# Twelve of sixteen batches with their transposes moved from TensorE to VectorE and DMA, one-instruction masked maxima, and regrouped slots

## The chip, the cores and the metric

The kernel runs on one core of a Trainium2 chip. A core has five instruction queues that run in parallel: TensorE (PE in the profile, with its weight loads as PEld), VectorE (DVE), ScalarE (ACT), GpSimd (POOL) and SyncE (SP). SP computes nothing; it issues the transfers (DMAs), which sixteen DMA engines then carry out. Each queue runs its instructions in the order in which they stand in the program and waits on semaphores for the others. The metric is the time of one execution in microseconds (us); lower is better.

## The reference

One layer is computed for sixteen batches of 256 tokens by 256 features, in float32. Reduced to its steps, per batch:

```
u    = modulate(layer_norm(logmap(x)))            # shift and scale from the condition vector
q,k,v = u @ Wqkv + b, rescaled per head (16 heads of 16 features)
o    = softmax(q k^T) v                           # full attention, 256 x 256 per head
x1   = mobius_add(x, gate * logmap(plin(o, Wo)))
u    = modulate(layer_norm(logmap(x1)));  ff = plin(plin(u, Wf1), Wf2)
xc   = mobius_add(x1, gate * ff)
local  = windowed attention on xc (64-token blocks, each sees itself and the block before)
remote = attention of 8 heads on 64 pooled tokens
xr   = x + (gate_l * local + gate_r * remote) @ Wout
z    = xr scaled per feature, @ W, scaled again
out  = xr + top-2 of 4 experts with low-rank updates on z (1024 hidden features)
```

The softmaxes of the local and the remote attention subtract the row maximum; the masks are additive.

## The kernel before

A batch is two tiles of 128 tokens (partitions) by 256 features. A matrix product needs its left operand with features in the partitions, so each product with a weight matrix is preceded by a transpose of the activation. `front(b)` computes up to `xc`, `back(b, xt, xc)` the rest; sixteen batches are unrolled in full.

**Who sets the order.** Nothing runs while the code is recorded: every call goes through the class `Plan`, which notes the instruction, its tiles and its predecessors as a node. `Plan.emit` then runs a list scheduler (`Plan.schedule`) over all nodes of all batches: each node has a cost from `Plan.cost`, a due time from its batch number times a period, and the scheduler gives each engine at each step the ready node with the earliest start, ties by due time. It also hands out the buffers (slots in SBUF under the tags t1, t2 and t4, eight PSUM banks). The result is a fixed order on each of the five queues, so batches overlap: the instructions of four to five batches stand interleaved. In TensorE's order of 5458 recorded operations, batch 7 reaches from 30% to 61% of the list.

**Transposes.** `turned(src, tag, b)` (line 699) makes four 128x128 TensorE transposes against `ident` into one PSUM bank, and `transposed` (line 708) copies the bank to SBUF, mostly on ScalarE. Per batch this is done eight times: `muT` twice (the two modulated inputs), `kT`, `qT`, `oT`, `xcT`, `locT` and `xrT`. The attention results come out as features by tokens in PSUM; `to_tokens` (lines 806 and 813) copies two banks to SBUF, one on VectorE and one on ScalarE, and transposes them back with eight TensorE transposes, for the full attention (`av`) and for the local one (`al`). The remote attention does the same with one bank and four transposes (lines 1120 and 1124). That is 32 + 16 + 4 = 52 TensorE transposes a batch.

**Local maxima.** For the row maxima of the local attention, TensorE first writes the mask into a bank, as a product of `ident_bf` with `maskq` (line 1046, sixteen a batch), then adds the scores on top of it (line 1048), and VectorE takes the maximum of two heads at a time with one TENSOR_REDUCE (line 1054, sixteen a batch).

**Transfers.** A batch issues 20 DMAs on SP: the input `x`, four pieces of the modulation vector `ada`, the row maxima through DRAM (`mT`: one write at line 1079, six reads at line 1083), the low-rank rows through DRAM (`low`: one write at line 1270, four reads at line 1273), the expert ratio `rho` through DRAM (line 1278 writes 256 elements of four bytes, line 1280 reads them back), and the output. The names carry over to the new kernel.

```
    def turned(src, tag, b):
        ps = bank(f"{tag}_ps_{b}").rearrange("p (c s) -> p c s", c=NC)
        for c in range(NC):
            for t in range(NT):
                pe.transpose(ps[:, c, bass.ts(t, P)], src[:, t, bass.ts(c, P)], ident)
```

Of the kernel before, what the change touches and what calls it, by code (L numbers as in the profile page):

```python
# [34 lines left out]
WIN = 64  # L35
E, R = 4, 4
# [8 lines left out]
N_T1, N_T2, N_T4 = 6, 18, 8  # L45
# [20 lines left out]
class Plan:  # L66
# [5 lines left out]
    PERIODS = 65.0, 70.0, 75.0, 80.0  # L72
    HURRIES = 5.0, 6.0, 7.0, 8.0
    early = ("pqk", "qk2")
    NARROWS = 3, 4

    def __init__(self, tc):
        nc = tc.nc
        self.tc, self.nodes, self.batch, self.hold = tc, [], 0, None
        self.seen, self.slots, self.ring, self.kept, self.wide = {}, {}, {}, set(), set()  # L80
        self.phys, self.place = {}, {}
        self.real = {"pe": nc.tensor, "dve": nc.vector, "act": nc.scalar, "pool": nc.gpsimd, "sp": nc.sync}
# [46 lines left out]
    def region(self, ap, write=False):  # L129
        name, dims = ap.name if isinstance(ap, View) else ap.tensor.name, list(ap.ap)  # L130
        if ap.space == DRAM and write:
            return name, 0, P, ap.offset, ap.offset + 1
        if ap.space in (PSUM, DRAM):
            return name, 0, P, 0, 1 << 30
        step = dims[0][0]
        p0, f0 = divmod(ap.offset, step)
        return name, p0, p0 + dims[0][1], f0, f0 + 1 + sum((n - 1) * st for st, n in dims[1:])

    def note(self, eng, op, args, kw):
# [7 lines left out]
        first = self.region(outs[0])[0]  # L147
# [4 lines left out]
        if not joins:  # L152
            n = dict(
                eng=eng, ops=[], cost=0.0, batch=self.batch, pre=set(), post=set(), tiles=set(),
                id=len(self.nodes), hold=self.hold, first=first, table=None, modes=[],
# [4 lines left out]
        n["cost"] += self.cost(eng, op, outs, rest, n)  # L160
        for write, aps in ((False, rest), (True, outs)):
            for ap in aps:
                if is_ap(ap):
                    self.access(n, write, *self.region(ap, write))
# [17 lines left out]
    def cost(eng, op, outs, rest, n):  # L182

        cols = max(int(np.prod(v.shape[1:])) for v in outs + [r for r in rest if hasattr(r, "tensor")])
        if eng == "sp":
            run = min((v.ap[-1][1] if v.ap[-1][0] == 1 else 1 for v in outs + rest if hasattr(v, "tensor")), default=1)
            return 0.1 + int(np.prod(outs[0].shape)) * 4 / (2e5 if run >= 128 else 0.7e5 if run >= 32 else 0.05e5)
        if eng == "pe":
# [8 lines left out]
            if n["hold"] is not None and (lhs.shape[0] < 64 or outs[0].shape[0] < 64):  # L197
                return (0.024 if lhs.shape[0] < 64 else 0.016) + 0.00042 * cols
# [7 lines left out]
        if eng == "pool":  # L206
            if op == "affine_select":
                return 0.2 + 0.00098 * cols
            return 0.76 if ALU.pow in rest else 0.27 + (0.0021 if op == "tensor_tensor" else 0.0009) * cols
        extra = 0.06 * (op == "scalar_tensor_tensor") + 0.05 * (op == "tensor_reduce") + 0.06 * (len(outs) > 1)  # L210
        return max(0.11, 0.05 + 0.0011 * cols + extra)


    def emit(self):
# [5 lines left out]
        for tag, names in self.ring.items():  # L220
            bufs = self.slots[names[0]][1]
            for old, new in zip(names, names[bufs:]):
                behind = [m["id"] for m in users[old]]
                for u in users[new]:
                    if tag in self.early and u["eng"] != "pe":
                        for m in [nodes[m] for m in u["pre"]]:
                            if m["eng"] == "pe" and m["batch"] == u["batch"]:
                                m["pre"].update(behind)
# [5 lines left out]
        lag = lambda n: {"pe": 0.27, "sp": 2.2, "dve": 0.18, "act": 0.18}.get(n["eng"], 0.05)  # L234
# [10 lines left out]
        settings = itertools.product(self.HURRIES, self.PERIODS, self.NARROWS)  # L245
        best = min(settings, key=lambda s: self.schedule(order, users, lag, *s)[0])
        _, out, self.place = self.schedule(order, users, lag, *best)
# [6 lines left out]
    def schedule(self, order, users, lag, hurry, period, most):  # L254
# [16 lines left out]
        held, narrow = set(), 0  # L271
# [4 lines left out]
        table, mode, out = None, None, []  # L276

        def start(n):
# [5 lines left out]
            for tag, names in need.items():  # L284
                if len(pools[tag]) < len(names):
                    return None, need
                if tag == "bank" and names[0] not in self.wide and narrow + len(names) > most:
# [4 lines left out]
        while len(out) < len(nodes):  # L292
            best = None
            for e, ns in avail.items():
                cand = [(max(t, free[e]), n, need) for n in ns for t, need in [start(n)] if t is not None]
# [26 lines left out]
            n["t"], n["end"] = t, end  # L322
            out.append(n)
# [6 lines left out]
            for m in n["post"]:  # L330
                m = nodes[m]
                m["ready"] = max(
                    m["ready"], end + (lag(n) if m["eng"] != e or e == "sp" else 0.08 if e == "dve" else 0.11 if e == "act" else 0.0)
# [8 lines left out]
def adaln_attn_ffn(ctx: ExitStack, tc: tile.TileContext, i: dict, out: bass.AP):  # L342
# [11 lines left out]
    def bank(name):  # L354
        return plan.tile(psum, [P, 512], "bank", name, 8, False)

    def four(name, b):

        banks = [bank(f"{name}{j}_{b}") for j in range(4)]
# [70 lines left out]
    def temp(shape, name, tag, bufs=1):  # L430

        return plan.tile(work, shape, tag, name, bufs, True, 2048)

    condT = const_tile([P, NC, B], "condT")
    load(condT, i["condT"].rearrange("(c p) b -> p c b", p=P))
    bada = temp([B, 6 * D], "bada", "qk2")
    load(bada, i["b_ada"].partition_broadcast(B))
    ada = temp([B, 6, D], "ada", "pqk")
    ada_f = ada.rearrange("b k d -> b (k d)")
    for k in range(3):  # L440
# [3 lines left out]
        load(wada, i["w_ada"][:, cols].rearrange("(c p) f -> p c f", p=P))  # L444
        for c in range(NC):
            pe.matmul(ps[:B, :], condT[:, c, :], wada[:, c, :], start=c == 0, stop=c == NC - 1)
        dve.tensor_tensor(ada_f[:, cols], ps[:B, :], bada[:, cols], ALU.add)
    for k in (1, 4):
        dve.tensor_scalar_add(ada[:, k, :], ada[:, k, :], 1.0)
    sp.dma_start(out=ada_dram, in_=ada_f)  # L450
# [11 lines left out]


    wf1 = temp([P, NC, FF], "wf1", "qk2")
    load(wf1, i["w_f1"].rearrange("(c p) f -> p c f", p=P))
    wf2 = temp([P, NF, D], "wf2", "qk2")
    load(wf2, i["w_f2"].rearrange("(c p) f -> p c f", p=P))
# [4 lines left out]
    for f in range(0, NF, 2):  # L472
        ps = bank(f"wf1T_ps{f}").rearrange("p (f d) -> p f d", f=2)
        for k in range(2):
            for c in range(NC):
                pe.transpose(ps[:, k, bass.ts(c, P)], wf1[:, c, bass.ts(f + k, P)], ident)
# [888 lines left out]
```

## Time and profile before

| | |
|---|---|
| median of three runs | 1300.51 us (1297.3 to 1302.75) |
| the profiled execution | 1302.17 us, its span 1300.4 us |
| granted TensorE clock, mean | 0.972 |
| TensorE busy | 1207.1 us, 93% |
| VectorE busy | 877.3 us, 67% |
| ScalarE busy | 688.2 us, 53% |
| GpSimd busy | 666.2 us, 51% |
| DMA engines busy, mean of 16 | about 12% |

The span runs from the first to the last instruction of the profiled execution; the execution's own time lies 1.8 us above it, and 1.7 us above the median of the runs. Busy time is the time in which an engine has at least one instruction running. The instructions of the output's store are recorded at 277.4, 353.9, 431.5, 500.0, 578.1, 646.6, 724.1, 792.6 and 873.7 us for the first batches, so a batch is finished every 75 us or so in the middle of the run.

### The profile page before, as it was taken

The page shows a single profiled execution, that of the slowest core. Times are in us where ns is not written, and L with a number is a line of the kernel's source. Part 1 is how long each engine was busy: PE and PEld are TensorE (multiplying, and loading weights), DVE is VectorE, ACT ScalarE, POOL GpSimd, SP SyncE. Part 2 cuts the span into 40 slices and gives each one's busy share as a digit, 9 for nine tenths or more (in the row PEclk, how much of TensorE's full clock was granted, in tenths as well). Part 3 has the DMA queues.
Part 4 walks back from the last instruction along what each step waited for, and adds up shares of the span by engine and source line. Part 5 has one row for each costly group of instructions (what it writes and reads, how often), then busy time and mean ns, then how long its engine had stood idle before and what let it go on. Part 6 is the DMA issues. An engine that isn't in the chain of part 4 may idle for free.

```text
span 1300.4 us, 27101 instructions
## 1 busy us (share of the span) xinstructions
PE 1207.1 (93%) x9684; PEld 797.8 (61%) x9684; DVE 877.3 (67%) x2800; ACT 688.2 (53%) x1750; POOL 666.2 (51%) x1677
## 2 busy tenths in 40 slices
PE   4987999999999999999999999999999998979776
PEld 2654565757666576657666576657656665757465
DVE  5747686876869677776869677676968765573331
ACT  1555667547473755647473755646473753724210
POOL 5167566646464564646464564656455462743210
PEclk7998999999999999999999999899999999999897
DMA  6520001010100201010100101020000100000001
GB/s 193 175 61 17 23 7 35 25 29 10 40 14 18 36 17 30 16 36 9 41 14 18 35 18 31 7 43 11 23 23 17 25 2 20 1 15 7 20 2 25
DMA packets 59462, 38.70 MB, mean 30 GB/s; under 512 B 33312, under 2 KB 53792, under 8 KB 59328
## 3 DMA queue, kind: packets, MB, share of 16 engines
q1 hardware_dynamic: 59328, 36.97, 11.6%
q8 instruction: 76, 1.25, 0.5%
q14 instruction: 58, 0.48, 0.1%
HBM read 31.60 MB, written 5.36 MB: 28 GB/s over the span
## 4 chain that ended last, share of the span: by engine, by line
PE 65%; DVE 11%; POOL 10%; ACT 6%; DMA 4%; issue 3%; SPq 0%; DVEq 0%; ACTq 0%; POOLq 0%
PE bank L784 11%; PE bank L1298 6%; PE bank L904 5%; PE bank L840 5%; PE bank L891 4%; PE bank L699 4%; PE bank L939 4%; PE bank L1048 3%; PE bank L1289 2%; PE bank L1211 2%; PE bank L1153 2%; POOL t L566 2%; PE bank L1046 2%; PE bank L974 2%; ACT t L662 2%
## 5 line engine op out<-in xcount | busy, mean ns | idle before, releaser
L566 POOL TENSOR_SCALAR_AFFINE_SELECT t<-t 128x512 f32<-128x512 f32 (+2 forms) x264 | 168.2, 661 | 37.7 <-ACT t L1174 36.8
L662 ACT ACTIVATE t<-t 128x256 f32<-128x256 f32 x224 | 92.8, 423 | 148.0 <-DVE t L733 53.4
L911 ACT ACTIVATE t<-bank 128x512 f32<-128x512 f32 x256 | 132.3, 615 | 38.8 <-PE bank L904 38.6
L784 PE MATMUL bank<-wot,t 128*128 128x256 f32 x512 | 129.2, 394 | 2.1 <-POOL t L1311 1.9
L1054 DVE TENSOR_REDUCE maxima<-bank 128x2 f32<-128x384 f32 (+1 forms) x256 | 119.9, 482 | 15.1 <-PE bank L1048 15.0
L1298 PE MATMUL bank<-t,wi 128*128 128x256 f32 x512 | 130.0, 389 | 0.0
L784 PEld LDWEIGHTS bank<-wot,t 128*128 128x128 f32 x512 | 93.2, 192 | 28.0 <-issue 11.8
L1174 ACT ACTIVATE t<-bank 128x320 f32<-128x320 f32 x256 | 92.9, 446 | 19.8 <-PE bank L1166 19.3
L1298 PEld LDWEIGHTS bank<-t,wi 128*128 128x128 f32 x512 | 91.5, 192 | 18.2 <-issue 9.0
L840 PE MATMUL bank<-wqkv,t 128*128 128x512 f32 (+1 forms) x256 | 94.8, 504 | 1.4 <-ACT t L708 1.4
L699 PE MATMUL bank<-ident,t 128*128 128x128 f32 x384 | 61.4, 284 | 18.0 <-DVE t L733 11.7
L904 PE MATMUL bank<-t,t 32*128 32x512 f32 x512 | 75.7, 646 | 0.1
L1311 POOL TENSOR_TENSOR t<-t,t 128x512 f32<-128x512 f32 x32 | 43.3, 1368 | 53.4 <-DVE t L1308 52.3
L891 PE MATMUL bank<-t,vpad 128*32 128x256 f32 x1024 | 68.3, 385 | 0.1
L699 PEld LDWEIGHTS bank<-ident,t 128*128 128x128 f32 x384 | 43.8, 142 | 39.2 <-DVE t L733 13.8
L844 DVE SCALAR_TENSOR_TENSOR pqk<-bank,m1f,bqkv 128x512 f32<-128x512 f32 (+1 forms) x64 | 38.9, 614 | 40.6 <-PE bank L840 31.2
L840 PEld LDWEIGHTS bank<-wqkv,t 128*128 128x128 f32 x256 | 45.7, 193 | 33.0 <-issue 25.2
L1166 PE MATMUL bank<-qk 32*128 32x128 f32 (+1 forms) x1024 | 58.9, 330 | 6.8 <-ACT t L1174 4.8
L1304 ACT ACTIVATE t<-bank 128x512 f32<-128x512 f32 x64 | 36.3, 593 | 53.1 <-PE bank L1298 53.1
L708 ACT COPY t<-bank 128x512 f32<-128x512 f32 x80 | 47.5, 593 | 31.6 <-PE bank L699 31.4
L1308 DVE SCALAR_TENSOR_TENSOR t<-bank,t 128x512 f32<-128x512 f32 x64 | 42.3, 681 | 29.9 <-PE bank L1289 29.7
L1166 PEld LDWEIGHTS bank<-qk 32*128 32x128 f32 x1024 | 45.4, 189 | 27.3 <-issue 12.3
(322 smaller groups left out, 2856.1 us busy)
## 6 DMA issues: line engine op xcount, KB each, us to landing
ada<-ada_dram SPq DMA_DIRECT2D x32, 256.0 KB
x<-in_x_dram SPq DMA_DIRECT2D x16, 256.0 KB
ada<-ada_dram SPq DMA_DIRECT2D x32, 128.0 KB
out_dram<-t SPq DMA_DIRECT2D x16, 256.0 KB
qk<-in_w_f_dram SPq DMA_DIRECT2D x2, 1024.0 KB
t<-low_dram SPq DMA_DIRECT2D x64, 32.0 KB
t<-rho_dram SPq DMA_DIRECT2D x16, 128.0 KB
t<-in_w_ada_dram SPq DMA_DIRECT2D x3, 512.0 KB
```

What stands on the lines that cost most here:

```text
L566: pool.affine_select(out=ap, in_=ap, pattern=pattern, compare_op=ALU.is_ge, fill=fill, base=base, channel_multiplier=cm,)
L662: act.activation(junk, src, AF.Square, accum_out=dst)
L699: pe.transpose(ps[:, c, bass.ts(t, P)], src[:, t, bass.ts(c, P)], ident)
L784: pe.matmul(ps[:, t, :], chunks[c][:, bass.ts(t, P)], weights[:, c, :], start=c == 0, stop=c == n - 1)
L840: pe.matmul(ps[:, :w], uT[:, c, bass.ts(t, P)], wqkv[:, c, a : a + w], start=c == 0, stop=c == NC - 1,)
L891: pe.matmul(avs[c][quad(j), gh, :], vpad[:, kt, head(2 * c + gh, j), :], es[j][:, gh, :], start=kt == 0 and gh == 0, stop=kt == NT - 1, sk ...
L904: pe.matmul(scs[j], kT[quad(j), c, bass.ts(kt, P)], qT[quad(j), c].rearrange("p g s -> p (g s)"), start=True, stop=True,)
L911: act.activation(es[j].rearrange("p g s -> p (g s)"), scs[j], AF.Exp)
L1054: dve.tensor_reduce(mx[:, qt, m0 : m0 + 4 * NC + 1 : 4 * NC], scs[j][:, : 2 * w].rearrange("p (g w) -> p g w", g=2), AX.X, ALU.max,)
L1166: pe.matmul(scs[j][:, a : a + w], k2T[quad(j), g % 2, g // 2, bass.ts(kt, P)], q2T[quad(j), g % 2, g // 2, kt * P : kt * P + w], start=Tru ...
L1174: act.activation(e[:, k, 0:NLOC], scs[2 * pr + k][:, :NLOC], AF.Exp)
L1298: pe.matmul(hs[j][:, f, :], wi[:, c, bass.ts(2 * j + f, P)], zT[:, c, :], start=False, stop=c == NC - 1, skip_group_check=True,)
```

## The change

What it does, in order of size:

1. **Transposes of batches 2 to 13.** For these twelve batches (`APART`) `transposed` no longer calls TensorE. VectorE transposes the tile in 32x32 blocks (one instruction, 128x512), four DMAs (one for each group of 32 partitions) write the blocks to a scratch matrix in DRAM in 128-byte runs, so that they lie in transposed order, and one DMA reads the matrix back into SBUF. `qT` and `xrT` take this way too. `to_tokens` and the remote attention's turn call the new `by_dram` for these batches: one VectorE block transpose straight from the PSUM bank, four DMA writes a bank, and one read for all banks. Batches 0, 1, 14 and 15 keep the TensorE transposes.
2. **Local maxima, in all batches.** The mask product is gone; VectorE makes one `tensor_tensor_reduce` a head and tile (scores plus mask, then maximum), 32 a batch in place of 16 TENSOR_REDUCEs. In the program each of these is two instructions, the main one and one that reads out the accumulator.
3. **Slots.** The input ring grows from 4 to 8 (`N_X`), t2 from 18 to 22 and t4 from 8 to 10 slots; the private rings `pqk`, `qk2`, `xpT`, `gkm`, `gkT`, `xr`, `p1o` and `p2o` are dissolved into these; small tiles have 3 or 6 buffers in place of 2. Products claim the SBUF slot of their result before they start.
4. **The planner.** It knows a DMA's issue cost (0.4 or 0.7 us) apart from its transfer time, allows eight DMAs under way, has other prices for VectorE, GpSimd and quarter-array products, follows regions of tiles more finely, and tries four settings. The DMAs of a batch rise from 20 to 83.

In the new order of TensorE's 4578 recorded operations, batch 7 reaches from 17.5% to 67% of the list.

```diff
+APART = range(2, 14)
-N_T1, N_T2, N_T4 = 6, 18, 8
+N_X = 8
+N_T1, N_T2, N_T4 = 6, 22, 10
...
+    SETTINGS = ((5, 55, 4, 1), (6, 65, 4, 0), (7, 75, 5, 1), (6, 65, 4, 1))
...
         if eng == "sp":
-            run = min((v.ap[-1][1] if v.ap[-1][0] == 1 else 1 for v in outs + rest if hasattr(v, "tensor")), default=1)
-            return 0.1 + int(np.prod(outs[0].shape)) * 4 / (2e5 if run >= 128 else 0.7e5 if run >= 32 else 0.05e5)
+            long = all(v.ap[-1][0] == 1 and v.ap[-1][1] >= P for v in outs + rest)
+            n["move"] = int(np.prod(outs[0].shape)) * 4 / (2.2e5 if long else 1.1e5)
+            return 0.4 if long else 0.7
...
+        if op == "tensor_tensor_reduce":
+            return 0.08 + 0.00105 * cols
...
             for e, ns in avail.items():
-                cand = [(max(t, free[e]), n, need) for n in ns for t, need in [start(n)] if t is not None]
+                since = free[e] if e != "sp" or len(landed) < 8 else max(free[e], landed[-8])
+                cand = [(max(t, since), n, need) for n in ns for t, need in [start(n)] if t is not None]
...
     def transposed(src, tag, b, copy=act.copy):
 
         t = spare([P, NC, S], tag, b)
-        copy(t, turned(src, tag, b))
+        if b in APART:
+            blocks = spare([P, NT, D // PADH, PADH], tag + "b", b)
+            dve.transpose(blocks.rearrange("p t k s -> p (t k s)"), src.rearrange("p t d -> p (t d)"))
+            rows = scratch([D, S], tag, b)
+            for a in range(4):
+                sp.dma_start(
+                    out=rows.rearrange("(k d) (t a s) -> d a t k s", d=PADH, a=4, s=PADH)[:, a],
+                    in_=blocks[quad(a)],
+                )
+            sp.dma_start(out=t, in_=rows.rearrange("(c p) s -> p c s", p=P))
+            return t
+        copy(t, turned(src, tag, b, t))
         return t
...
+    def by_dram(banks, tag, b):
+        n = 4 * len(banks)
+        rows = scratch([2 * S // PADH, PADH, n, PADH], tag, b)
+        for c, ps in enumerate(banks):
+            t = spare([P, 2 * S // PADH, PADH], f"{tag}c{c}", b)
+            dve.transpose(t.rearrange("p k r -> p (k r)"), ps.rearrange("p g s -> p (g s)"))
+            for j in range(4):
+                sp.dma_start(out=rows[:, :, 4 * c + j].rearrange("k s r -> s k r"), in_=t[quad(j)])
+        o = spare([P, 2, NT, n, PADH], tag + "o", b)
+        sp.dma_start(
+            out=o.rearrange("p g t n r -> p (g t) (n r)"),
+            in_=rows.rearrange("(m k) s n r -> (k s) m (n r)", k=4),
+        )
+        return [o[:, :, t].rearrange("p g n r -> p n g r") for t in range(NT)]
+
+    def to_tokens(banks, tag, b, into):
+        if b in APART:
+            return by_dram(banks, tag, b)
...
                 with plan.unit():
-                    for j in range(4):
-                        pe.matmul(scs[j][:, : 2 * w], ident_bf, maskq[:, 2 * a : 2 * (a + w)], start=True, stop=False)
                     for j in range(4):
                         pe.matmul(
                             scs[j][:, : 2 * w], qm[quad(j), c, bass.ts(qt, P)], km[quad(j), c, :, k0 : k0 + w],
-                            start=False, stop=True,
+                            start=True, stop=True,
                         )
                 for j in range(4):
-                    m0 = 4 * c + j
-                    dve.tensor_reduce(
-                        mx[:, qt, m0 : m0 + 4 * NC + 1 : 4 * NC],
-                        scs[j][:, : 2 * w].rearrange("p (g w) -> p g w", g=2), AX.X, ALU.max,
-                    )
+                    for gh in range(2):
+                        m = 4 * (NC * gh + c) + j
+                        dve.tensor_tensor_reduce(
+                            out=seen[:, :w], in0=scs[j][:, gh * w : (gh + 1) * w], in1=maskf[:, a : a + w], scale=1.0,
+                            scalar=NEG, op0=ALU.add, op1=ALU.max, accum_out=mx[:, qt, m : m + 1],
+                        )
...
-        rT = spare([P, LG, S], "avrc", b)
-        dve.tensor_copy(rT, avr)
+        if b in APART:
+            pss = by_dram([avr], "avr", b)
...
-        ps = turned(xr, "xrT", b)
+        if b in APART:
+            ps = xsT = transposed(xr, "xrT", b)
```

## The prediction

> **What bounds the kernel now.** I read the busy shares first, then the slices, then the busy times by stretch, then the groups that the change touches, then SP's queue.
>
> ```profile
> PE 1207.1 (93%) x9684; PEld 797.8 (61%) x9684; DVE 877.3 (67%) x2800; ACT 688.2 (53%) x1750; POOL 666.2 (51%) x1677
> PE   4987999999999999999999999999999998979776
> DVE  5747686876869677776869677676968765573331
> ...
> PE 65%; DVE 11%; POOL 10%; ACT 6%; DMA 4%; issue 3%; SPq 0%; DVEq 0%; ACTq 0%; POOLq 0%
> ```
>
> TensorE is full except at both ends, and 65% of the chain that ended last is TensorE's own work. The stretches (us busy and, in brackets, instructions) show it in numbers:
>
> ```profile
> core 0: us, PE busy (x) PEld busy (x) DVE busy (x) ACT busy (x) POOL busy (x), PEclk, DMA share, GB/s
> 0.00:300.00 300.00, 259.61 (x1894) 161.25 (x1894) 214.00 (x702) 165.65 (x415) 162.41 (x438) 0.95 0.22 62
> 300.00:976.00 676.00, 661.99 (x5472) 436.74 (x5470) 491.94 (x1566) 394.26 (x1013) 377.44 (x954) 0.99 0.11 23
> 976.00:1300.40 324.40, 285.54 (x2322) 199.81 (x2320) 171.38 (x534) 128.29 (x324) 126.31 (x286) 0.94 0.07 13
> ```
>
> The middle 676 us are nine batch periods of 75.1 us (output stores every 75 us). Per period TensorE is busy 73.6 us (98%), VectorE 54.7 (73%), ScalarE 43.8, GpSimd 41.9. The two ends hold the other seven batches' worth of work and 79 us of idle TensorE. So TensorE work removed in the middle is worth its full length, until VectorE, next in line with 20 us to spare, takes over. The groups touched:
>
> ```profile
> L699 PE MATMUL bank<-ident,t 128*128 128x128 f32 x384 | 61.4, 284 | 18.0 <-DVE t L733 11.7 <-DVE m2ay L691 3.3 <-ACT t L881 0.9
> L813 PE MATMUL bank<-ident,t 128*128 128x128 f32 x256 | 40.9, 278 | 0.6 <-ACT t L881 0.5
> L1124 PE MATMUL bank<-ident,t 128*128 128x128 f32 x64 | 12.7, 285 | 0.2 <-DVE t L1120 0.2
> L1054 DVE TENSOR_REDUCE maxima<-bank 128x2 f32<-128x384 f32 x128 | 67.8, 547 | 9.9 <-PE bank L1048 9.9
> L1054 DVE TENSOR_REDUCE maxima<-bank 128x2 f32<-128x256 f32 x128 | 52.1, 417 | 5.2 <-PE bank L1048 5.1
> L806 DVE COPY t<-bank 128x512 f32<-128x512 f32 x32 | 22.1, 691 | 43.0 <-PE bank L891 23.3 <-PE bank L1153 19.8
> ```
>
> Here the first number after the bar is the group's busy time, the second one instruction's length. Last, the transfers: a stretch in which almost only 128-byte runs are moved, one in which one 256 KB input of 1 KB runs is loaded, and SP's wait at the four-byte writes of `rho`:
>
> ```profile
> 430.50:432.00 1.50, 1.50 (x20) 0.57 (x23) 0.88 (x2) 0.52 (x3) 1.05 (x6) 1.00 0.31 50
> 409.00:410.50 1.50, 1.50 (x17) 0.95 (x15) 1.50 (x7) 0.00 (x0) 0.00 (x0) 1.00 0.67 175
> SPq L1280 <- DMA rho_dram<-rtx: 94.0, 15, 8.2
> ```
>
> **The change part by part.** *TensorE, transposes.* Three groups of line 699 (61.4 + 12.8 + 10.6 us for 512) give 0.166 us each; line 813 gives 0.160, line 1124 0.198. A batch of the twelve loses 32 x 0.166 + 16 x 0.160 + 4 x 0.198 = 8.7 us. *TensorE, masks.* Line 1046 is 46.5 us in all, 2.9 us a batch, gone in all sixteen. So TensorE needs 73.6 - 11.6 = 62.0 us for a batch of the twelve and 70.7 for the other four.
>
> *VectorE, block transposes.* Thirteen a batch of 128x512. The trace has this operation at 128x64 only: 0.245 us (the low-rank rows). With the slope of the TENSOR_REDUCE rows, (547 - 417)/128 = 1.02 ns a column, 448 more columns make 0.70 us, as the 512-column copy's 0.69: +9.1 us. Gone are four such copies (-2.7); splitting six tiles' products adds about 0.6.
>
> *VectorE, maxima.* No row has this operation. The nearest has two inputs, a 256-column product with an accumulator (line 745), at 0.42 us, followed by an accumulator read of 0.081 us. Down the same slope, 128 columns cost 0.29 and 192 cost 0.35; with the read 0.37 and 0.43. Sixteen of each make 12.9 us against 119.9/16 = 7.5 now: +5.4 us in every batch. From below, without the read, 10.3 (+2.8); from above, two inputs at twice the slope, 17.9 (+10.4). I take +5.4, by the two rows that are nearest. The planner prices the two forms at 0.21 and 0.28 us, so its order leaves VectorE too little room.
>
> Sum for VectorE: 54.7 + 9.1 - 2.7 + 0.6 + 5.4 = **67.1 us** for a batch of the twelve, 60.7 for the others. That passes TensorE's 62.0: the bound moves to VectorE. ScalarE loses five copies of 0.593 and two of 0.587 us, to 39.7; GpSimd stays.
>
> *SP.* 52 writes and 11 reads are added. The low-rank reads, also 32 partitions in 128-byte runs, take 0.604 us to issue, the `mT` write 0.32; inputs 0.39. So 16.6 to 31.4 us for the writes (I take the upper, the like shape) and 4.3 for the reads, beside 9.0 now: 45 us a batch. SP stands still, too: `rho`'s read waits for `rho`'s write, 94.0 us in 15 times, 6.3 each. Before, few were in a hurry behind it; now block writes and reads of other batches are. About 5 us a batch, as a few issues fit in between: 50 of 70 us, not the bound.
>
> *DMA engines.* 13 x 2048 runs of 128 bytes. In the first stretch 50 GB/s x 1.5 us are 75 KB, 586 runs, in 0.31 x 16 x 1.5 = 7.4 engine-us: 12.7 ns a run. That is for reading DRAM; the writes have no row. From above: all 59328 packets of the queue, 11.6% of 16 x 1300 us, mean 40.7 ns. The writes take 26624 x 12.7/16 = 21 us a batch, or 68 at the upper end; thirteen reads of 256 KB cost 0.67 x 1.5 = 1.0 us each; 0.11 x 75 = 8 are there now. So 42 us (89 at the upper end); I take 42, since the 256-byte writes of `mT` let their reads go 1.8 us after issue, no slower than reads.
>
> A rule speaks against this. The Trainium skill, "VectorE: DVE Perf Modes", section "The three transpose paths", says that a plain copy which transposes by strides is 19 times slower than the hardware's transpose; taken at 19 x 1.0 us for each of thirteen tiles that would be an estimated 247 us of DMA a batch, and a time near 3400 us. But there single elements are scattered; here VectorE has turned the 32x32 blocks and the runs stay 128 bytes long. By the rule the prediction fails outright; by the row it stands.
>
> *Latency.* A turn through DRAM takes 0.7 (VectorE) + 2.4 (four issues) + 1.8 (landing, as `mT`) + 0.4 + about 2.2 us (landing of a read) = 7.5, and about 6 more when ten other DMAs stand between on SP, as is typical. Nine such turns follow one another in a batch. What covers it is the order: between a block transpose and the first user of its result stand, in the median by kind of turn, 13 to 34 us of TensorE work and 11 to 38 of VectorE work by the rows above, and each batch now spans half the list. At the shortest distances (4 to 6 us in `alo`, `locT`, `xcT`) an engine will wait. *Slots* cost nothing by themselves: they are what allows eight batches under way. Extra `x` loads at the start lie among 190 GB/s of weight loads.
>
> **The sum.** Middle: nine periods. VectorE at 67.1 us cannot be as full as TensorE was (98%), since TensorE stands at 62.0 beside it and SP's order ties batches together. Bounds: 67.1/0.98 = 68.5, and 75.1 if all is lost. I take 95%, 70.6 us, nearer the first: 9 x 4.5 = 40 us less. Ends: VectorE is idle for 86 and 153 us there, so TensorE still paces them; four batches without the new path gain 2.9 each and three with it 11.6: 46 us less. The idle 79 us stay. 1300.4 - 40 - 46 = 1214; the execution's 1.8 us on top and the 1.7 us by which it lies above the median cancel. **1215 us.** A change within 0.5% (6.5 us) could not be told from none.
>
> **Rivals.** *TensorE stays the bound.* VectorE's 50 us of extra work at the ends fit its idle time; if the order spreads its work so well that the middle runs at TensorE's 62.0/0.98 = 63.3 us, 9 x 11.8 + 46 = 152 less: 1148; at VectorE's mean over all batches, 65.5/0.98 = 66.8, it is 1180. For it speaks the eight-batch depth, against it the planner's low VectorE prices.
>
> *The turns come late.* A stream of 63 more DMAs, held up each batch for about 8 us at `rho`, stalls the engines until the period is 75 again: 1255 if the ends keep their gain, 1300 if the longer batch latency eats that too.
>
> *The short writes bind (slower).* DMA work a batch is 21 us + 1.66 us for each nanosecond of a 128-byte write. It passes VectorE's 67 us at 28 ns and today's 75 at 32 ns. At the 40.7 ns above it is 89 us: 9 x 14 more in the middle, the three batches at the ends +14 each, less 12 from the other four: 1456. For it: four-byte writes hold `rho`'s read 6.3 us for 256 elements, 0.4 us for each of an engine's sixteen. Against it: the 256-byte writes show nothing of the kind, and 128 is nearer to them.
>
> **How the numbers follow.** VectorE-paced 0.50 (1190 to 1250), TensorE-paced 0.22 (1148 to 1190), late turns 0.13 (1250 to 1300, a third of it within 0.5% or above), short writes 0.15 (from 1310 up). The range leaves out most of the last case and the lower end of the second: 1150 to 1310. Faster 0.50 + 0.22 + 0.08 = 0.80, same 0.03, slower 0.17.
>
> **What would show it.** VectorE busy near 1050 us (877 + 16 x 6.0 + 12 x 6.4) and TensorE near 1057 in a span near 1214; the maxima's main instruction at 0.29 and 0.35 us with an accumulator read of 0.08; the block transpose at 0.70; output stores 70 us apart; a DMA share near 0.6 in the middle; a chain in which VectorE has gained on TensorE, with waits for `muT`, `av` and `al` through DRAM of a few us a batch. Block transposes of 0.9 us, maxima of 0.5, a DMA share over 0.9, or TensorE waiting mostly for SP's reads would make it wrong.

## The result, and the profile after

| | before | after |
|---|---|---|
| median of the runs | 1301.45 us | 1382.38 us (1381.05 to 1387.42) |
| ratio, 95% interval | | 1.0635 (1.0598 to 1.0671) |
| span of the profiled execution | 1300.4 us | 1385.7 us |
| granted TensorE clock, mean | 0.972 | 0.909 |
| TensorE / VectorE busy | 1207.1 / 877.3 us | 1201.2 / 984.3 us |

The forecast was 1215 us in a range of 1150 to 1310. The change makes the kernel 6.4% slower: size and sign were wrong.

The page of the changed kernel: busy time, two rows of slices and the chain that ended last.

```profile
PE 1201.2 (87%) x8799; PEld 781.2 (56%) x8804; DVE 984.3 (71%) x3754; ACT 661.3 (48%) x1676; POOL 653.8 (47%) x1677
...
PE   4997977888998988898899889988988989898886
...
DVE  5896898688768879685887869777836385583631
...
q1 hardware_dynamic: 434080, 118.81, 39.2%
...
PE 36%; DVE 28%; DMA 12%; POOL 10%; issue 6%; ACT 6%; SPq 2%; DVEq 0%; ACTq 0%; POOLq 0%
```

The row of nines that TensorE had in the middle is gone, and nothing has taken its place: VectorE stands at 71%, the DMA engines at 39% (the share at the end of the queue's line). The chain passes from engine to engine: TensorE's own work is 36% of it, 65% before. By this page no single engine bounds the kernel; it waits in turn for each.

The same three stretches as in the prediction (the last is longer by the time lost):

```profile
core 0: us, PE busy (x) PEld busy (x) DVE busy (x) ACT busy (x) POOL busy (x), PEclk, DMA share, GB/s
0.00:300.00 300.00, 239.19 (x1460) 138.36 (x1460) 237.06 (x917) 168.77 (x427) 166.90 (x492) 0.88 0.48 121
300.00:976.00 676.00, 608.04 (x4718) 390.03 (x4721) 528.75 (x1981) 347.42 (x889) 349.54 (x885) 0.93 0.49 101
976.00:1386.00 410.00, 353.98 (x2624) 252.84 (x2624) 218.50 (x858) 145.07 (x362) 137.36 (x300) 0.89 0.19 39
```

In the middle TensorE falls from 98% to 90%, VectorE rises to 78%, and the granted clock falls from 0.99 to 0.93. The first output is stored at 359 us (277 before), the second at 476 (354), the eighth at 944 (793): the middle wins nothing back, it loses 29 us more from the second store to the eighth. The last is stored at 1382 us (1297).

I cut TensorE's time into three parts, from its instructions and the clock records of the trace: work at full clock (busy time less half of the busy time that lies in stretches at half clock), what the half clock adds, and idle time up to TensorE's last instruction (the span ends some 4 us later).

| | span | work at full clock | added by half clock | idle |
|---|---|---|---|---|
| before | 1300.4 | 1184 | 23 | 89 |
| after | 1385.7 | 1099 | 102 | 180 |
| difference | +85 | -85 | +79 | +91 |

So the change does take work off TensorE, 85 us of the 151 that the prediction counted (12 x 8.7 + 16 x 2.9), but order and clock cost twice that. The groups that the change made, and the two score groups beside them:

```profile
L1132 DVE CUSTOM_DVE_ANT_0 seen<-bank,maskf 128x128 bf16<-128x128 f32 (+1 forms) x512 | 165.3, 323 | 45.9 <-PE bank L1125 9.5 <-PE bank L1218 0.5 <-DVE maxima L1132 0.2
L976 PE MATMUL bank<-t,t 32*128 32x512 f32 x512 | 92.6, 697 | 19.2 <-DVE t L912 6.0 <-ACT t L951 5.2 <-DVE maxima L1132 4.4
L1125 PE MATMUL bank<-t,t 32*128 32x256 f32 (+1 forms) x512 | 79.3, 512 | 16.9 <-DVE maxima L1132 8.8 <-DVE maxima L1150 3.0 <-ACT t L1300 1.8
L743 DVE STREAM_TRANSPOSE t<-t 128x512 f32<-128x512 f32 x96 | 66.7, 699 | 2.5 <-PE bank L1068 1.2 <-PE bank L1393 0.7
L855 DVE STREAM_TRANSPOSE t<-bank 128x512 f32<-128x512 f32 x60 | 42.5, 708 | 36.8 <-PE bank L961 15.5 <-PE bank L1193 14.5 <-DMA al_dram<-t 3.2
L1132 DVE DVE_READ_ACCUMULATOR2_ANT maxima<- 128x1 f32 x512 | 42.3, 83 | 0.3
```

The prices were right: block transposes 0.70 us, maxima 0.323 in the mean (0.290 and 0.356 by shape) and 0.083 for the accumulator read. In the kernel before the two score groups had these rows:

```profile
L904 PE MATMUL bank<-t,t 32*128 32x512 f32 x512 | 75.7, 646 | 0.1
L1048 PE MATMUL bank<-t,t 32*128 32x256 f32 (+1 forms) x512 | 52.5, 480 | 0.0
```

The rows grew by 16.9 and 26.8 us, some of it by the half clock: together nearly the 46.5 us of the mask products' row. And TensorE now waits 19.2 and 16.9 us before them.

### The profile page after: what moved, and what is told of

Read it like the earlier page. It is cut to its first block, busy times and chain, and to the rows that moved or that the text cites. A ratio compares the mean times of both kernels' runs of the same rounds, so it can differ in the third digit from the quotient of the medians.

```text
span 1385.7 us, 27800 instructions
## 1 busy us (share of the span) xinstructions
PE 1201.2 (87%) x8799; PEld 781.2 (56%) x8804; DVE 984.3 (71%) x3754; ACT 661.3 (48%) x1676; POOL 653.8 (47%) x1677
## 4 chain that ended last, share of the span: by engine, by line
PE 36%; DVE 28%; DMA 12%; POOL 10%; issue 6%; ACT 6%; SPq 2%; DVEq 0%; ACTq 0%; POOLq 0%
PE bank L828 7%; DVE seen L1132 6%; PE bank L1393 5%; PE bank L976 3%; PE bank L1125 3%; DMA t<-xcT_dram 3%; POOL t L605 2%; PE bank L961 2%; DVE t L743 2%; DMA t<-mT_dram 2%; DMA t<-low_dram 2%; PE bank L908 2%; PE bank L1384 2%; DVE t L1402 2%; PE bank L1253 2%
## 5 line engine op out<-in xcount | busy, mean ns | idle before, releaser
L605 POOL TENSOR_SCALAR_AFFINE_SELECT t<-t 128x512 f32<-128x512 f32 (+1 forms) x260 | 166.2, 666 | 92.7 <-ACT t L1261 91.6
L1132 DVE CUSTOM_DVE_ANT_0 seen<-bank,maskf 128x128 bf16<-128x128 f32 (+1 forms) x512 | 165.3, 323 | 45.9 <-PE bank L1125 9.5
L1393 PE MATMUL bank<-t,wi 128*128 128x256 f32 x512 | 121.0, 387 | 0.0
L976 PE MATMUL bank<-t,t 32*128 32x512 f32 x512 | 92.6, 697 | 19.2 <-DVE t L912 6.0
L1125 PE MATMUL bank<-t,t 32*128 32x256 f32 (+1 forms) x512 | 79.3, 512 | 16.9 <-DVE maxima L1132 8.8
L1253 PE MATMUL bank<-t,t 32*128 32x192 f32 (+1 forms) x1024 | 65.4, 352 | 17.7 <-ACT t L1261 6.7
L1253 PEld LDWEIGHTS bank<-t,t 32*128 32x128 f32 x1024 | 50.3, 206 | 44.3 <-issue 15.4
L855 DVE STREAM_TRANSPOSE t<-bank 128x512 f32<-128x512 f32 x60 | 42.5, 708 | 36.8 <-PE bank L961 15.5
L743 DVE STREAM_TRANSPOSE t<-t 128x512 f32<-128x512 f32 x96 | 66.7, 699 | 2.5 <-PE bank L1068 1.2
L1238 PE MATMUL bank<-t,v2pad 128*32 128x128 f32 (+1 forms) x1536 | 54.5, 270 | 9.7 <-POOL t L605 4.2
```

The costliest lines, as they stand in the source:

```text
L605: pool.affine_select(out=ap, in_=ap, pattern=pattern, compare_op=ALU.is_ge, fill=fill, base=base, channel_multiplier=cm,)
L743: dve.transpose(blocks.rearrange("p t k s -> p (t k s)"), src.rearrange("p t d -> p (t d)"))
L976: pe.matmul(scs[j], kT[quad(j), c, bass.ts(kt, P)], qT[quad(j), c].rearrange("p g s -> p (g s)"), start=True, stop=True,)
L1125: pe.matmul(scs[j][:, : 2 * w], qm[quad(j), c, bass.ts(qt, P)], km[quad(j), c, :, k0 : k0 + w], start=True, stop=True,)
L1132: dve.tensor_tensor_reduce(out=seen[:, :w], in0=scs[j][:, gh * w : (gh + 1) * w], in1=maskf[:, a : a + w], scale=1.0, scalar=NEG, op0=ALU. ...
L1253: pe.matmul(scs[j][:, a : a + w], k2T[quad(j), g % 2, g // 2, bass.ts(kt, P)], q2T[quad(j), g % 2, g // 2, kt * P : kt * P + w], start=Tru ...
```

## The experiments

Three things can be blamed: the turns through DRAM, the maxima, and the new planner with its slots, which settles the order on every engine anew. All times below are medians, with the ratio to the kernel before measured beside it (it took 1299 to 1305). A setting of the planner is given as hurry (how heavily waiting times weigh in the due times), period in us, the number of PSUM banks that short products may hold and, in the new planner, how many fewer of them the later batches may.

### The parts, one taken out at a time

x1: the turns out; maxima, planner and slots stay (the planner takes setting 6, 65, 4, 0).

```diff
-APART = range(2, 14)
+APART = range(0)
```

> No batch has its transposes made by VectorE and DMA; the one-instruction maxima, the new slots and the new planner stay (the planner now picks hurry 6, period 65). If the turns through DRAM are what costs the time (late arrivals, and the half clock that follows the gaps), this runs below the kernel before: 1300 minus the 46 us of mask products, about 1255, with a granted clock of 0.96 or more. If the maxima on VectorE are the cause, it stays above 1320. If the new slots and planner are, it stays above 1320 as well, and the first output store stays near 359 us.

1379.91 us, ratio 1.062 (1.059 to 1.065): without the turns the kernel is as slow, at another setting, so the turns alone do not explain the loss.

x2: the maxima out; turns, planner and slots stay (setting 7, 75, 5, 1).

```diff
+                        pe.matmul(scs[j][:, : 2 * w], ident_bf, maskq[:, 2 * a : 2 * (a + w)], start=True, stop=False)
...
-                    for gh in range(2):
...
+                    dve.tensor_reduce(
+                        mx[:, qt, m0 : m0 + 4 * NC + 1 : 4 * NC],
```

> The maxima are made as before (mask product on TensorE, sixteen TENSOR_REDUCEs a batch), the turns through DRAM stay (the planner picks hurry 7, period 75). If the 32 short VectorE instructions that hold the score banks are the cause, about 1240 to 1290 (TensorE has 46 us more work than in the changed kernel, VectorE 88 less). If the turns are, 1370 or more.

1343.31 us, ratio 1.034 (1.026 to 1.041): 39 us better, still worse than before.

x3: both out, so that planner and slots are left. None of the four settings gives a complete order here, so five were added; 7, 75, 3, 0 was taken.

> Neither the turns through DRAM nor the new maxima: the kernel before with the new slots and the new planner alone. None of the four settings gives a complete order here, so five more are offered; the planner picks hurry 7, period 75, three narrow banks. If slots and planner do no harm, 1290 to 1310. If the new order by itself costs time (a late first batch, more gaps), 1330 or more.

1391.12 us, ratio 1.071 (1.067 to 1.074). Of the slots the prediction says that they "cost nothing by themselves"; with the planner that comes with them, this order costs 90 us. Its waits of TensorE (line waited for, releaser: us, times, longest):

```profile
PE bank L1189 <- DMA t<-mT_dram: 27.7, 6, 8.9
PE bank L1258 <- DMA t<-mT_dram: 17.2, 4, 6.7
PE bank L1389 <- DMA t<-low_dram: 16.4, 3, 12.2
```

These transfers were in the kernel before, too, where TensorE waited 17.6 us for `mT` and 10.7 for `low`; in the new order it reaches their users too early and waits 44.9 and 16.4.

x5: after, at the setting that x2 took.

```diff
-    SETTINGS = ((5, 55, 4, 1), (6, 65, 4, 0), (7, 75, 5, 1), (6, 65, 4, 1))
+    SETTINGS = ((7, 75, 5, 1),)
```

> The changed kernel with the planner held to hurry 7, period 75, five narrow banks, in place of the 5, 55, four that it chose: the same instructions in another order. If the choice of the order is what fails (the dues of a 55 us period start eight batches at once, so the first output store comes at 359 us instead of 277), 1230 to 1300 with a first store before 300 us. If the turns or the maxima fail whatever the order, within 2% of 1382.

1401.94 us, ratio 1.079 (1.073 to 1.084). At one and the same setting the maxima cost 59 us over x2.

### The parts put into the kernel before

y1: the new maxima alone, with the old planner and slots (which now takes setting 8, 75, 4).

> The kernel before with the one-instruction maxima alone; old planner, old slots. If the new planner and slots alone make the loss (the kernel before with them took 1391 us), the maxima bring what was forecast for them, less what VectorE's 5.4 us a batch give back: 1250 to 1285. If the maxima hurt in any order, 1300 or more.

1366.23 us, ratio 1.046 (1.041 to 1.052).

y2: the turns alone with the old planner and slots (only one setting, 5, 75, 3, gives an order).

> The kernel before with the turns through DRAM for batches 2 to 13 alone; old planner (it prices the short writes at 70 GB/s and knows no limit of eight DMAs), old slots. If planner and slots make the loss, the turns bring most of the 104 us of TensorE transposes: 1200 to 1245. If the turns come late in any order, 1280 or more.

1582.85 us, ratio 1.212 (1.206 to 1.218).

```profile
PE bank L796 <- DMA t<-locT_dram: 38.9, 8, 8.3
PE bank L1192 <- POOL t L567: 32.3, 30, 5.4
PE bank L796 <- DMA t<-oT_dram: 31.5, 3, 20.5
PE bank L700 <- DVE t L745: 30.3, 7, 12.3
```

With the old slots the turns are plainly late: TensorE waits up to 20.5 us for one of them. So the new slots and planner together make the turns bearable (the prediction gave this to the slots; which of the two does it was not taken apart), but that is not their whole effect.

y3: turns and maxima with the old planner and slots (setting 5, 65, 3).

> Both in the kernel before, with its own planner and slots: the change without its parts 3 and 4. If those two parts make the loss, this is the forecast's own case, with VectorE as the bound: 1150 to 1250. If turns and maxima together fail in any order, 1300 or more.

1600.19 us, ratio 1.227 (1.222 to 1.232).

### Is it the order itself?

z1 and z2: the kernel before, with nothing changed but its planner's setting. It takes 7, 75, 4 by itself.

```diff
-    PERIODS = 65.0, 70.0, 75.0, 80.0
-    HURRIES = 5.0, 6.0, 7.0, 8.0
-    NARROWS = 3, 4
+    PERIODS = (70.0,)
+    HURRIES = (6.0,)
+    NARROWS = (3,)
```

> The kernel before with nothing changed but the setting of its own planner: hurry 6, period 70, 3 narrow banks in place of 7, 75, 4 (both belong to its 32 settings). Every instruction is the same; only the fixed order on the engines differs. If the order itself carries the loss (theory), another order of the same work lands away from 1300: 1330 to 1400, with TensorE's idle time above 120 us (89 before) and more stretches at half clock. If all orders of the old planner are about as good, and it is the new slots and claims that cost 90 us (rival), 1290 to 1315 with idle time of 80 to 100 us.

1294.71 us, ratio 0.993 (0.990 to 0.996).

z2 has 75, 8 and 4 in these three lines.

> The same with hurry 8, period 75, 4 narrow banks, which is the setting that the old planner took once the new maxima were in (that kernel took 1366). Theory (the order carries the loss): most of those 66 us is the setting, so 1340 to 1380 with the old maxima still in. Rival (the maxima themselves cost it, by VectorE's load): 1295 to 1320.

1364.31 us, ratio 1.046 (1.040 to 1.052). This is the time of y1 to within 2 us, with the old maxima in it: the "cost of the maxima" in y1 is no more than what the setting, which the planner took with them, costs alone. Neither theory is right for both kernels. Orders of the same work do scatter, by 70 us, but a good one is not unique. The middle stretch of z1, then of z2:

```profile
300.00:1000.00 700.00, 686.65 (x5784) 472.05 (x5777) 511.31 (x1653) 399.34 (x1042) 394.80 (x996) 1.00 0.11 24
```

```profile
300.00:1000.00 700.00, 654.20 (x5284) 437.86 (x5285) 482.95 (x1519) 398.96 (x971) 364.68 (x907) 0.96 0.10 22
```

In z2 TensorE is idle for 46 us there (13 in z1), and the clock is at 0.96 in place of 1.00. So gaps are paid twice, as idle time and by the slower clock that follows them.

### What in the planner makes the bad order?

x6: after, with the old planner's prices for quarter-array products, GpSimd and VectorE (setting 5, 55, 4, 1, as in after).

```diff
-                return (0.02 if lhs.shape[0] < 64 else 0.006) + 0.00042 * cols
+                return (0.024 if lhs.shape[0] < 64 else 0.016) + 0.00042 * cols
...
-            return 0.65 if ALU.pow in rest else 0.15 + (0.0021 if op == "tensor_tensor" else 0.0009) * cols
+            return 0.76 if ALU.pow in rest else 0.27 + (0.0021 if op == "tensor_tensor" else 0.0009) * cols
```

> The changed kernel with the planner's old prices for quarter-array products, GpSimd and VectorE; its SP model, settings, claims and slots stay, and it picks the same setting (5, 55, four). If the new prices make the bad order, 1230 to 1310. If the claims, the slots or the rest of the planner do, within 2% of 1382.

1420.73 us, ratio 1.088 (1.083 to 1.094): no help with turns and maxima both in.

w1: after, with prices set to the durations in its trace.

> The kernel after with the planner's prices set to the durations that its trace shows (maxima 0.32 + 0.083, transposes 0.136, small GpSimd operations 0.25, small VectorE operations 0.13, powers 0.73, matmuls some 8 per cent up), and setting 5, 60, 4, 0, at which this planner's own plan is shortest. If wrong prices are what made the order bad (theory A), TensorE's idle time falls from 180 to under 130 us and the time to 1300 to 1345. If the list planner cannot find a tight order with the new slots whatever its prices (theory B), 1365 to 1420, idle time 160 us or more.

1390.97 us, ratio 1.066 (1.061 to 1.071); TensorE idle 186 us. True prices do not mend it: theory A falls for this kernel.

w2: the same with the maxima as before.

> The same prices with the maxima as before (turns through memory, new planner and slots), setting 6, 70, 4, 0. Against 1343 of the same kernel by the planner's own prices. Theory A: 1280 to 1325. Theory B: 1335 to 1390.

1373.95 us, ratio 1.053 (1.047 to 1.058), 31 us worse than with the change's own, falser prices (and another setting). A price list that is nearer to the trace does not by that make a better order.

v1: x3 (neither turns nor maxima) with all prices and lags of the old planner, its DMA prices included, and without the limit of eight DMAs; setting 7, 70, 4, 1. Slots and claims are the new ones.

```diff
-    NEXT = {"pe": 0.0, "dve": 0.12, "act": 0.11, "pool": 0.14, "sp": 2.0}
+    NEXT = {"pe": 0.0, "dve": 0.08, "act": 0.11, "pool": 0.0, "sp": 2.2}
...
-        lag = lambda n: {"pe": 0.27, "sp": 2.0, "dve": 0.18, "act": 0.18, "pool": 0.16}[n["eng"]]
+        lag = lambda n: {"pe": 0.27, "sp": 2.2, "dve": 0.18, "act": 0.18}.get(n["eng"], 0.05)
...
-                since = free[e] if e != "sp" or len(landed) < 8 else max(free[e], landed[-8])
+                since = free[e]
```

> The kernel with neither turns nor maxima (new planner and slots alone: 1391 us), with the planner's prices, lags and distance of dependent instructions put back to those of the kernel before, setting 7, 70, 4, 1. New slots, claims, lists of freed tiles and the limit on later batches stay. Theory P (the new planner's prices and lags make the bad order): 1285 to 1325, TensorE idle under 115 us. Theory S (the new slots and the claims do it, whatever the prices): 1365 to 1410, idle 140 us or more.

1322.94 us, ratio 1.017 (1.015 to 1.020). Between these two orders, prices, lags and the limit (with the setting that goes with them) are 68 of the 90 us that planner and slots cost alone; 22 are left for slots, claims and the luck of the order.

v2: the turns with the old prices of the four engines (and the new price and limit of the DMAs), setting 7, 70, 4, 0.

> Turns through memory with the maxima as before, new slots and claims (1343 us by the new prices, 1374 by prices from the trace), with the old planner's prices of the four engines and their lags, the new price of a DMA, setting 7, 70, 4, 0. Theory P: 1250 to 1300, so that it may beat the kernel before. Theory S: 1335 to 1385.

1310.00 us, ratio 1.008 (1.005 to 1.011).

v3: turns and maxima, priced in the same way, setting 7, 80, 4, 0.

> The same with the new maxima too (all of the change but the planner's prices of the four engines; the maxima priced at 0.31 and 0.38 us), setting 7, 80, 4, 0. Theory P: 1280 to 1330. Theory S: 1370 to 1420.

1391.29 us, ratio 1.069 (1.064 to 1.074). Theory P holds for v1 and comes close for v2; for v3 it fails, by 60 us and more.

### The maxima beside the turns

u1: the fourth corner, maxima without turns, priced as v2, setting 5, 55, 4, 1.

> The fourth corner beside v1, v2 and v3: new slots and claims, the old planner's prices of the four engines, the new maxima but no turns, setting 5, 55, 4, 1. If the maxima hurt in every order (theory M: 16 instructions a batch more, the score banks held longer, VectorE's queue fuller), it takes 1365 to 1400, some 45 to 80 us over the 1323 without them, as 1391 stands over 1310 with the turns in. If the 81 us of v3 were the luck of one order (theory L), 1310 to 1345.

1311.00 us, ratio 1.008 (1.004 to 1.011). Without the turns the maxima cost nothing in this order; it is 12 us faster than v1.

u2: the turns alone in a second order of the same instructions, by setting 6, 70, 3, 0 and shifted due times.

```diff
-            n["due"] = n["batch"] * period - n["tail"]
+            n["due"] = n["batch"] * period - n["tail"] + 0.005 * ((n["id"] * 7919 + seed * 104729) % 997)
```

> The turns alone (1310 us) in a second order: the due time of every step is shifted by up to 5 us by its number, setting 6, 70, 3, 0. Same instructions. It says how far one order stands for the part: within 15 us of 1310 if the part decides; if orders scatter as 1295 and 1364 of the kernel before did, 1275 to 1370. Under 1295 it would beat the kernel before.

1292.38 us, ratio 0.9925 (0.9900 to 0.9951). It is 6.5% faster than after and a little faster than the kernel before. But z1, a free choice of setting, is as fast without any of the change.

u3: turns and maxima in a second order, setting 5, 60, 3, 0.

> Turns and maxima (1391 us by setting 7, 80, 4, 0) in a second order of the same prices, setting 5, 60, 3, 0. Theory M: 1370 to 1410, TensorE idle 170 us or more. Theory L: 1300 to 1350.

1377.00 us, ratio 1.057 (1.053 to 1.060). Both orders are bad, so theory L falls here.

The four corners with the old prices and the new slots (v1 alone has the old DMA prices, too, and no limit of eight), TensorE's time cut as above, and what it waited for VectorE (all rows of its waits whose releaser is VectorE, summed):

| | time | work at full clock | added by half clock | idle | waits for VectorE |
|---|---|---|---|---|---|
| neither (v1) | 1323 | 1171 | 33 | 114 | 30 |
| maxima (u1) | 1311 | 1170 | 40 | 94 | 35 |
| turns (v2, u2) | 1310, 1292 | 1116, 1101 | 48, 49 | 144, 136 | 37, 16 |
| both (v3, u3) | 1391, 1377 | 1093, 1096 | 99, 98 | 193, 180 | 61, 59 |

Each part alone gains 12 to 31 us; together they lose 54 to 68 against neither. Gains of that size are less than the scatter of orders (z1 and z2), and v1 and u1 are one order each. By the change's own prices the corners are 1391 (neither, x3), 1380 (maxima, x1), 1343 (turns, x2) and 1382 (both): there both still gain 9 us against neither, but 50 less than the two parts added up. The maxima take hardly any work off TensorE, 1 us without the turns and 5 to 23 with them. Once the turns are there, they double what the half clock costs, and add 44 to 49 us of idle time (u2 to u3, v2 to v3). VectorE's work in the middle stretch is 489 us (v1), 531 (u1), 552 (u2) and 561 (u3) of 700. The waits of u3 (TensorE, then its weight loads), where the maxima now stand among the first:

```profile
PE bank L1384 <- DMA t<-low_dram: 23.2, 7, 12.7
PE bank L1184 <- DMA t<-mT_dram: 16.0, 3, 6.4
...
PE bank L976 <- DVE maxima L1132: 8.7, 5, 2.8
...
PE bank L1125 <- DVE maxima L1132: 7.7, 12, 1.6
```

```profile
PEld bank L1125 <- DVE maxima L1132: 23.7, 41, 2.2
```

The rows of TensorE's waits for the maxima come to 0.7 us in u2 and 14.1 in v2, to 26.8 in u3 and 32.2 in v3. The banks of the scores wait for a VectorE that has 208 us of maxima to make in place of 109, and 109 us of block transposes beside them. Six kernels with both and the new slots took 1377, 1382, 1391, 1391, 1402 and 1421 us; four with the turns alone took 1292, 1310, 1343 and 1374. Pair by pair the maxima cost 59 us at one setting (x2, x5), 67 to 99 by the old prices, and 17 by the prices from the trace (w2, w1). So in every pair tried the maxima cost time beside the turns, and each of the six is slower than each of the four, though w2 and u3 lie only 3 us apart; how much the clash costs is blurred by the scatter of the orders. Whether they clash by VectorE's load or by the score banks, held longer under eight short instructions and their accumulator reads than under four, was not taken apart. What a still better planner could do with both is open, too.

## Why the prediction was wrong

**The prices were right.** Block transpose 0.699 and 0.708 us (forecast 0.70); maxima 0.290 and 0.356 (0.29 and 0.35); accumulator read 0.083 (0.081); a 128-byte run 12.4 ns by the packets' records (12.7), and a DMA share of 0.49 in the middle (near 0.6). The rival of the short writes is out. The prediction also weighed a rule from the Trainium skill, "VectorE: DVE Perf Modes", section "The three transpose paths": a factor of 19 for a copy that transposes by strides. The page states it against the DMA engines' own transpose and for a large innermost stride at the destination. The blocks that VectorE has turned are written in 128-byte runs, which is not that case; at 12.4 ns a run the trace shows nothing of the factor.

**The sum, set against the trace.** 1214 us with TensorE busy for 1057 means 157 us of idle time; measured are 1201 and 185 (to the end of the span). The miss of 172 us in the span is thus mostly in TensorE's busy time: 66 us of work that did not go (85 of 151), 79 us by the half clock, and 27 us more idle time.

**The step that failed** is "VectorE at 67.1 us cannot be as full as TensorE was (98%) ... I take 95%". VectorE is 78% full in the middle, and output stores there stay some 76 us apart. The 98% of the kernel before is not a property of the work: z2, the same instructions at another setting of its own planner, has TensorE at 93% in the middle and takes 1364 us. The prediction carried that tightness over to an order that was made anew. "*Slots* cost nothing by themselves" is the same step in words: planner and slots got no price, and x3 puts them at 90 us (v1, with the old prices, at 22). The prediction did see that the planner prices the maxima at 0.21 and 0.28 us, "so its order leaves VectorE too little room", and drew no number from it; w1, with true prices, is no faster, so that one price is not the whole cause.

**The half clock was left out.** Every sum was made at the clock of before. But a VectorE-paced kernel is one in which TensorE has many small gaps, and these are paid twice: 102 us in after, 23 before. The likeliest case was too cheap even by its own logic.

**Masks: mis-sized.** "46.5 us in all, gone" was read from this row of the kernel before:

```profile
L1046 PE MATMUL bank<-maskq,ident_bf 128*128 128x384 bf16 (+1 forms) x256 | 46.5, 300 | 1.9 <-ACT t L708 0.9 <-DVE t L1193 0.8 <-DVE maxima L1054 0.2
```

It is the time in which at least one mask product runs, and products of other rows overlap it. By the trace's records only 33.8 of the 46.5 us had a mask product alone on TensorE. And the score products took some of that back: from v1 to u1 the score rows of the full and the local attention rose from 77.8 and 52.5 us to 90.5 and 64.0. Work at full clock fell by 1 us in all; with the turns in, by 5 and 23.

**Transposes: mis-sized, too.** 8.7 us a batch were to leave TensorE, 104 us in all. The same reading was too high here: the groups of lines 699, 813 and 1124 together are busy for 136.4 us, but for only 83.9 of them with nothing else on TensorE. That is 5.2 us a batch, or an estimated 63 for the twelve. From v1 to v2 and u2, work at full clock falls by 54 and 70, and the time by 13 and 31, since idle time and half clock take the rest. The rival "turns come late" named this mechanism (TensorE waits for `mT`, `low` and `locT` among the first), but ended at 1300.

**"Ends: 46 us less; the idle 79 us stay."** They hold most of the loss: the second output is stored 122 us later than before, the eighth 151, and the last batches win 66 of it back.

**The rival that was missing** is a slower kernel in which no engine and no queue is saturated. The only one priced above 1310 needed saturated DMA engines.

## What to carry to other kernels

When a list scheduler fixes the order, its new order is a part of the change and may cost more than all the work removed: before you blame a part, run the old kernel at a second setting, and each part in at least two orders. A kernel in which TensorE is 98% busy can only lose tightness, so count idle time and half clock as terms of the sum. Two edits that each shift work to the same second engine may each gain and together gain much less, or lose, long before that engine is full. And a row's busy time is not what TensorE saves without it: take off what other rows overlap.

## What the runs showed of the hardware

**The half clock needs no idle window.** In after there are 42 stretches at half clock, 253 us in all; before had 10 with 73 us. In after all but the last, which the end cuts, last a multiple of 3.41 us (3.4, 6.8, 10.2 or 13.7), and all begin on one grid of that step. Of its windows on this grid at full clock, 4 had next to no TensorE work and were followed by half clock, but so were 24 of the 25 that were less than half busy, 8 of the 21 that were 50 to 70% busy, and 5 of the 276 above that. Four neighbouring stretches of after, each 3.4 us:

```profile
461.90:465.30 3.40, 2.34 (x23) 1.36 (x21) 3.01 (x15) 1.17 (x4) 0.88 (x1) 1.00 0.05 10
465.30:468.70 3.40, 2.29 (x25) 1.98 (x26) 3.40 (x7) 0.52 (x2) 3.12 (x5) 1.00 0.05 10
468.70:472.10 3.40, 3.40 (x8) 1.03 (x10) 3.23 (x14) 2.17 (x8) 2.73 (x6) 0.50 0.45 78
472.10:475.50 3.40, 3.40 (x20) 1.09 (x16) 3.19 (x18) 2.44 (x7) 1.97 (x7) 1.00 0.40 84
```

TensorE is busy for 2.34 and 2.29 us of the first two (69% and 67%), and the clock (the number after the last bracket) is halved in the third, in which it has nothing but work. The longest gap that the timeline shows there is 1.25 us. The Trainium skill, "TensorE: Matmul & The Clock Gate", in its Part 1 on the HAM clock gate, gives windows of about 3.4 us, which agrees, and puts the fall of the clock after at least one idle window, which does not: here windows with work in them were enough. The busy share does not settle it alone: of the 9 windows at 60 to 70%, 7 were not followed by half clock.

**The score products' rows grow without their instructions growing.** Taking the mask products out (from v1, the first three lines, to u1, the last three) leaves the mean length of a score product as it was, 661 and 653 ns, 480 and 483, and yet their rows are busy for longer:

```profile
L978 PE MATMUL bank<-t,t 32*128 32x512 f32 x512 | 77.8, 661 | 7.6 <-DVE t L754 4.3 <-ACT t L953 1.9 <-DVE t L914 0.8
L1129 PE MATMUL bank<-t,t 32*128 32x256 f32 (+1 forms) x512 | 52.5, 480 | 0.0
L1127 PE MATMUL bank<-maskq,ident_bf 128*128 128x384 bf16 (+1 forms) x256 | 45.9, 301 | 3.2 <-DVE t L1405 1.7 <-DVE maxima L1135 1.2 <-ACT t L754 0.3
...
L976 PE MATMUL bank<-t,t 32*128 32x512 f32 x512 | 90.5, 653 | 3.8 <-DVE maxima L1132 2.2 <-ACT t L981 0.8 <-DVE t L752 0.3
L1125 PE MATMUL bank<-t,t 32*128 32x256 f32 (+1 forms) x512 | 64.0, 483 | 11.3 <-DVE maxima L1132 6.8 <-ACT t L1053 2.4 <-DVE maxima L1150 0.8
PEld bank L1125 <- DVE maxima L1132: 22.7, 41, 1.7
```

What changed are the starts. At full clock the four local score products that go to four banks start within 20 ns of one another in v1; in u1 their starts spread over 141 ns in the mean. In v1 the mask products stand in front of them and take the wait for the banks; in u1 the score products wait themselves, and the row of their weight loads (the last line) names the maxima, 41 times. The full attention's row does not always follow: without turns but with the new maxima it is 77.9 us in x1, against 84.3 in x3 with the old.
